# Preparing late weights as planned steps beside group 0, with per-tile waits on released pools

## The chip, the cores and the metric

One Trainium2 chip; the program runs on one of its NeuronCores. The metric is the device time of one execution in microseconds. Before the change the runs gave 2528.05, 2527.34 and 2525.23 us, a median of 2527.34.

A core has five engines that work beside each other, each with its own queue of instructions taken in order: TensorE (PE, matmuls and transposes; PEld is its weight load), VectorE (DVE), ScalarE (ACT), GpSimd (POOL) and SyncE (SP, which here only issues transfers). SPq, ACTq and POOLq in the profile are the issuing sides of SP, ACT and POOL.

## What is computed

Two layers over x of 64 graphs with 256 nodes and 256 features, all in fp32:

```python
x = x + gat(layernorm(x), adj, L0_gnn_W, L0_gnn_a)          # masked softmax attention over the nodes
x = x + mamba2(layernorm(x), W_in, conv, dt, A, D, norm_w, W_out, W_lin, b_lin)
x = x + rgcn(layernorm(x), adj, L1_gnn_weight, L1_gnn_bias) # sums over neighbours, by relation
x = x + moe(layernorm(x), gate_w, gate_b, w1, b1, w2, b2)   # best of 8 experts, capacity 1.25
```

What matters below is the weights. The kernel does not use them as they come. It takes the mean over rows out of W and W_in (so that a layer norm's mean drops out), multiplies the router's weights gate_w, and the columns of W_in that give dt, into the weights of each layer (so that the router's logits and dt come along as a few more columns of products that are made anyway), and folds norm_w, W_out and W_lin into one matrix.

## The kernel before

**First pass.** 16384 tokens are worked on in 32 groups of 512 (two graphs each). A group runs through `attention`, `scan`, `mix` and `relate`; after two groups, `choose` routes their tokens and scatters a record of each into a list in DRAM, `slots`. At its end, two full blocks of the mixture of experts are computed beside the last groups (`first_block`), and `list_blocks` lists the rest. x after the third sum goes to DRAM (`x3d`). **Second pass.** The blocks of the experts that are left are run, in three kinds: quarters (128 tokens), halves (256) and wholes (512), each with its own 1 MB of w1 and of w2. `fetch_slots` reads a block's records, `gather` brings its tokens' rows by indirect transfer from POOL, `fetch_weights` loads the weights, `turned` transposes the rows, `experts` computes. Two blocks' records of each kind and the first block's weights are asked for at once when the pass begins.

**The order within the first pass** is planned in Python while the program is built. `Plan.step` takes an engine, an estimate of its time, a function that issues the instructions, and what it reads and writes. `Plan.record` then simulates the five engines: again and again it picks the step that can begin first, and issues it. Among steps of one engine that can begin within 0.05 us of each other, the lower rank goes first; the rank is `PACE * group + due`, with one due time for each step of a group (`DUE`), and one for each step of the end (`LATE`). The instructions of each engine go out in exactly this order (`manual_schedule`). A tile asked for through the plan (`Plan.tile`) has a number of buffers in turn; a step that needs a buffer waits until all steps of its last use are issued. `AtOnce` has the same interface and issues every step on the spot; a second form of the kernel, for adjacency matrices with entries above 1, is written with it and does not run on this input.

**Preparation of the weights** stands ahead of the plan, in plain program order, in pools of its own, `prep` and `prep_ps` (L514). Its parts, with the lines of the profile:
- ACT issues the load of W_in into `win` (L445) and of small vectors; SP issues the other loads.
- `centred` (L476) takes means out: two products with a matrix of ones, two steps on DVE. It is used for gate_w and the dt columns of W_in (together `gq`), W (`wx`), the three parts of `win`, and the relation's weights (`wrel`).
- `projected` (L488) multiplies a matrix by `gq`: two transposes, a copy (L497), a product (L500), a copy (L504), for each half. It is used for W, `wrel` and W_lin (`wl`).
- Products of W with the attention vectors a (L556, L557), the bias columns (L540), W_out transposed (`woT`, L572) and multiplied by `wl` into `wf` (L579, L583), and b1 transposed and stored in DRAM as `b1d` (L588 to L591).

Attention needs `wx`, `scan` needs `win` and the bias `blin`, `mix` needs `wf`, `relate` needs `wrel` and `brel`, and the expert blocks need `b1d`. When `prep` closes, its memory is released; `fast_pool` and `fast_ps` (L1424), in which all tiles of the first pass lie, are opened over it. In the same way the pools of the second pass (`et`, `es`, `eps`, L1464) are opened over those of the first, the weights' pool `wts` among them. Where a pool is opened over a released one, the first access to it waits for the released pool's last.

Of the kernel before, what the change touches and what calls it, by code (L numbers as in the profile page):

```python
# [31 lines left out]
PACE = 4.60  # L32
DUE = [
    -187, -691, -72, 159, -113, -114, -149, 636, 174, 171, 387, 756, -229, -1087, -1172, 20, -351,
    -599, 699, -611, -1484, 249, -770, -710, -1048, 376, -331, 864, -405, 61, -28, 134, 16, -9,
    348, 442, -429, -1102, -42, 703, -223, 113, -607, 108, 990, 202, 295, 646, 26, 263, -92, 233,
    247, -557, -374, -723, 667, 329, -360, -253, -391, -1223, -304, -600, -778, -988, -488, -62,
    -720, -720, -306, -566, -4, 261, -344, 153, -232, -603, -36, -391, 947, 502, -439, -94, -126,
    29, -246, 327, -208, -945, 61, -486, -490, -648, -49, 120, 553, 10, -408, -1120, -935, -301,
    -1702, 164, -515, 586, -50, -355, 132, 744, -80, 96, -1, 160, -115, 422, 133, 217, -609, 128,  # L40
    -1196, 106, -198, -115, -589, -56, 549, -876, -729, 476, -280, -741, -486, -186, -114, 171,
    711, -911, -300, -262, 1079, -444, -107, -98, 127, 135, -372, -12, -97, 504, 638, 342, -669,
    -318, 1, 363, -806, -1604, -646, -790, 276, -140, 264, -165, 370, 251, 14, -435, -518, -133,
    -470, -615, 98, 237, -148, -214, -868, -1044, -884, 125, 722, 505, 627, 310, 101, 280, 264,
    947, 409, -79, 138, -8, -1018, -924, -303, -515, -328, -216, -660, 755, 133, 127, -181, 129,
    -683, -19, 86, -697, 353, 242, -391, 243, -479, -626, 320, 328, 221, -542, -377, 191, 161,
    -181, 223, -433, -295, 139, 127, 151, -181, 152, -496, -30, 178, -458, 330, 615, -10, 301,
    198, -168, 566, 303, -1378, -203, 504, -349, 138, 15, 93, -300, -469, -71, -1080, -905, -382,
    -765, -499, 522, -559, -436, -711, -1062, -307, -489, 705, -263, 262, 48, 538, -87, -172, -7,
    -532, -975, -688, -187, -1308, -570, 302, -1059, -506, 779, 83, -11, 749, -4, 216, 469, 900,  # L50
    -1142, 86,
]
LATE = [
    439, 482, 387, 262, 460, 193, 260, 587, 397, 193, 239, 309, 207, 431, 312, 489, 501, 247, 320,
    397, 398, 341, 500, 377, 575, 532, 367, 505, 283, 139, 276, 464, 345, 243, 455, 107, 575, 200,
    296, 296, 296, 296, 296, 296, 296, 296, 296, 296, 296, 296, 170, 321, 356, 486, 13, 179, 363,
    192, 357, 768, 395, 1857, 2047, 1812, 2046, 1886, 2036, 1982, 2016, 1957, 1976, 1757, 1937,
    1678, 2042, 1873, 2052, 2162, 2018, 2061, 1964, 2122, 1809, 397, 1880, 2090, 446, 466, 2153,
    1801, 208, 1845, 1887, 420, 371, 1753, 2084, 343, 1955, 1982, 469, 302, 1752, 1929, 128, 2080,
    1921, 332, 270, 332, 389, 145, 449, 139, 514, 497, 334, 177, 408, 502, 1660, 1834, 1843, 1988,  # L60
    2202, 2247, 2273, 2186, 2179, 1985, 1853, 1933, 1944, 2220, 1882, 2133, 1815, 2009, 2179,
    2095, 1789, 1828, 563, 1802, 1733, -146, 109, 1792, 2073, 414, 1763, 1943, 143, 509, 2344,
    2010, 508, 2033, 2085, 250, 423, 2196, 2256, 716, 2018, 1585, 411, 176,
# [56 lines left out]
class Plan:  # L120
# [20 lines left out]

    def tile(self, tag, shape, dtype=F32, bufs=1):
        home = Home(self.pool, tag, shape, dtype, bufs)
        line = self.tags.setdefault(tag, [])

        home.before = (line[-1] if line else None, line[-bufs] if len(line) >= bufs else None)
        line.append(home)
        return home
# [11 lines left out]
    def step(self, engine, us, go, reads, writes, late=0.0):  # L160
        k = self.k.get(self.due, 0)
        self.k[self.due] = k + 1
        due = (DUE if self.due == "group" else LATE)[k]
# [124 lines left out]
def gnn_mamba_rgcn_moe(ctx: ExitStack, tc: tile.TileContext, a: dict, out: bass.AP):  # L288
# [143 lines left out]
    def first_pass(form, pass1):  # L432
# [12 lines left out]
        nc.scalar.dma_start(out=win, in_=a["L0_ffn_W_in"].rearrange("(k p) o -> p k o", p=P))  # L445
# [30 lines left out]
        def centred(pool, banks, dst, src, n):  # L476

            ps = banks.tile([P, 512], F32, tag="ps0", name="ps")
            for k in range(2):
                nc.tensor.matmul(  # L480
                    ps[:, :n], lhsT=ones_pp, rhs=src[:, k, :], start=(k == 0), stop=(k == 1)
                )
            for k in range(2):
                nc.vector.scalar_tensor_tensor(
                    dst[:, k, :], ps[:, :n], -1.0 / D, src[:, k, :], ALU.mult, ALU.add
                )

        def projected(pool, banks, dst, src, n):  # L488

            for k in range(2):  # L490
                ps = banks.tile([P, 512], F32, tag="ps0", name="ps")
                for o in range(2):
                    nc.tensor.transpose(
                        ps[:, o * P : (o + 1) * P], src[:, k, o * P : (o + 1) * P], ident
                    )
                srcT = pool.tile([P, 2 * P], F32, tag="srcT", name="srcT")
                nc.vector.tensor_copy(srcT, ps[:, : 2 * P])  # L497
                ps = banks.tile([P, 512], F32, tag="ps0", name="ps")
                for o in range(2):
                    nc.tensor.matmul(  # L500
                        ps[:, :n], lhsT=srcT[:, o * P : (o + 1) * P], rhs=gq[:, o, :n],
                        start=(o == 0), stop=(o == 1),
                    )
                nc.vector.tensor_copy(dst[:, k, :], ps[:, :n])  # L504

        def relation(pool, banks, dst, r):

            nc.sync.dma_start(
                out=dst[:, :, 0:D], in_=a["L1_gnn_weight"][r].rearrange("(k p) o -> p k o", p=P)
            )  # L510
            centred(pool, banks, dst[:, :, 0:D], dst[:, :, 0:D], D)
            projected(pool, banks, dst[:, :, D:DG], dst[:, :, 0:D], E + 1)

        with tc.tile_pool(name="prep" + form, bufs=1) as prep, tc.tile_pool(  # L514
            name="prep_ps" + form, bufs=2, space=PSUM
        ) as prep_ps:
            own = prep, prep_ps

            w0 = prep.tile([P, 2, D], F32, name="w0")
            nc.sync.dma_start(out=w0, in_=a["L0_gnn_W"].rearrange("(k p) o -> p k o", p=P))  # L520
            gq0 = prep.tile([P, 2, E + 1 + NH], F32, name="gq0")
            nc.vector.memset(gq0[:, :, E : E + 1], 0.0)
            nc.sync.dma_start(
                out=gq0[:, :, 0:E], in_=a["L1_ffn_gate_w"].rearrange("(k p) e -> p k e", p=P)
            )
            nc.vector.tensor_copy(gq0[:, :, E + 1 :], win[:, :, DPROJ - NH :])
            centred(*own, gq, gq0, E + 1 + NH)
            nc.vector.memset(gq[:, :, E : E + 1], -1.0 / D)
            centred(*own, wx[:, :, 0:D], w0, D)
            projected(*own, wx[:, :, D:DQ], wx[:, :, 0:D], E + 1 + NH)  # L530
            for o in range(0, DPROJ - NH, 512):
                part = win[:, :, o : min(o + 512, DPROJ - NH)]
                centred(*own, part, part, min(512, DPROJ - NH - o))
            relation(*own, wrel[:, 0], 0)
            for vec, dst in (("L0_ffn_b_lin", blin), ("L1_gnn_bias", brel)):
                col = prep.tile([P, 2], F32, tag="col", name="col", bufs=2)
                nc.sync.dma_start(out=col, in_=a[vec].rearrange("(k p) -> p k", p=P))
                ps = prep_ps.tile([P, 512], F32, tag="ps0", name="ps")
                for k in range(2):
                    nc.tensor.matmul(  # L540
                        ps[:, : E + 1], lhsT=col[:, k : k + 1].to_broadcast([P, P]),
                        rhs=gq[:, k, : E + 1],
                        start=(k == 0), stop=(k == 1),
                    )
                nc.vector.tensor_copy(dst[:, D:DG], ps[:, : E + 1])

            av = prep.tile([P, 2, D], F32, name="av")
            for i in range(2):
                nc.sync.dma_start(
                    out=av[:, i, :],  # L550
                    in_=a["L0_gnn_a"][i * D : (i + 1) * D, :].rearrange("d o -> o d").broadcast_to([P, D]),
                )
            prod = prep.tile([P, 4, D], F32, name="prod")
            for k in range(2):
                for i in range(2):
                    nc.vector.tensor_mul(prod[:, 2 * k + i, :], wx[:, k, 0:D], av[:, i, :])  # L556
# [1114 lines left out]
```

## Time and profile before

| | us |
|---|---|
| median of 3 runs | 2527.34 |
| profiled execution, its own time | 2531.42 |
| its span (first to last instruction) | 2529.7 |
| PE busy | 2366.6 (94%) |
| DVE busy | 1918.0 (76%) |
| ACT busy | 1641.0 (65%) |
| POOL busy | 826.1 (33%) |

The span is cut into 40 slices of 63 us; a digit is the busy share of a slice in tenths. The last rows are the clock that TensorE was granted, and the DMA engines:

```profile
PE   5899999999999999999999999999884899999996
...
PEclk8999999999999999999999999999997999999998
DMA  3212222322222232222232222222417433333332
```

The first slice and slices 29 to 31 (1830 to 1960 us) differ from the rest. They are the start, and the step from the first pass to the second.

Lines of the timeline give the start, the busy time, the engine, the line of code, the operation with what it writes and reads, the sizes, and in brackets the idle time of the engine just before with what ended it. Rows by stretch give start:end, its length, busy time with number of instructions by engine, the granted clock, the share of the DMA engines' time and GB/s.

### The profile page before, as it was taken

How to read it: one execution, taken by the hardware profiler on the slowest of the kernel's cores; microseconds unless marked ns; L12 is line 12 of the kernel's file. 1: busy time of each engine (PE TensorE's matmuls, PEld its weight loads, DVE VectorE, ACT ScalarE, POOL GpSimd, SP SyncE). 2: the span in 40 equal slices, each digit the busy share in tenths (PEclk: the TensorE clock that was granted, in tenths of full speed). 3: DMA queues.
4: the chain of work that ended last, by engine and by line, in shares of the span. 5: the costliest groups of instructions: out<-in, count | busy, mean ns of one | idle time of the engine just before them, and what ended most of it. 6: DMA issues, size and time to landing. Idle time of an engine off the chain costs nothing.

```text
span 2529.7 us, 35024 instructions
## 1 busy us (share of the span) xinstructions
PE 2366.6 (94%) x11451; PEld 1652.4 (65%) x11451; DVE 1918.0 (76%) x4825; ACT 1641.0 (65%) x3720; POOL 826.1 (33%) x762
## 2 busy tenths in 40 slices
PE   5899999999999999999999999999884899999996
PEld 4567766667667666766766676676654666666664
DVE  3899999999989899999999999999762243344433
ACT  1878888878888787888888888787522223232331
POOL 1122424333342433334343333432523222222231
PEclk8999999999999999999999999999997999999998
DMA  3212222322222232222232222222417433333332
GB/s 113 45 22 57 58 63 62 77 56 53 62 54 70 60 75 54 54 62 64 61 76 57 53 62 53 70 58 44 134 34 264 139 119 116 122 112 108 127 112 64
DMA packets 173527, 198.93 MB, mean 79 GB/s; under 512 B 25448, under 2 KB 157870, under 8 KB 173312
## 3 DMA queue, kind: packets, MB, share of 16 engines
q1 hardware_dynamic: 124816, 135.70, 16.6%
q0 software_dynamic: 46816, 58.88, 12.6%
q8 instruction: 98, 1.61, 0.3%
q10 hardware_dynamic: 1680, 1.79, 0.2%
q14 instruction: 117, 0.96, 0.1%
HBM read 112.47 MB, written 45.45 MB: 62 GB/s over the span
## 4 chain that ended last, share of the span: by engine, by line
DVE 32%; issue 30%; PE 16%; POOL 10%; ACT 8%; DMA 3%; POOLq 0%; SPq 0%; ACTq 0%; DVEq 0%
PE ps L744 11%; DVE y L963 8%; POOL rs L752 4%; POOL xg L409 3%; POOL out_dram L427 3%; DVE gate L946 3%; DVE gate L1108 2%; DVE xh L1105 2%; DMA xg<-x3d,place 2%; DVE st L760 2%; DVE dm L1088 2%; PE ps L1095 1%; DVE ev L857 1%; DVE bm L973 1%; DVE ev L859 1%
## 5 line engine op out<-in xcount | busy, mean ns | idle before, releaser
L744 PE MATMUL ps<-xnT,win 128*128 128x512 f32 x1152 | 542.0, 600 | 4.0 <-ACT xnT L786 4.0
L963 DVE SCALAR_TENSOR_TENSOR y<-ps,cw,y 128x510 f32<-128x510 f32 (+2 forms) x480 | 351.5, 739 | 5.1 <-ACT y L956 3.9
L1030 ACT ACTIVATE dm<-ps,cs 128x256 f32<-128x256 f32 (+1 forms) x1024 | 334.4, 477 | 23.4 <-PE ps L744 22.6
L752 POOL TENSOR_TENSOR rs<-ve,mhalf 128x4 f32<-128x4 f32 x96 | 157.8, 1644 | 562.7 <-DVE ve L750 439.3
L744 PEld LDWEIGHTS ps<-xnT,win 128*128 128x128 f32 x1152 | 204.6, 190 | 170.8 <-issue 157.0
L1563 PE MATMUL ps<-xnT,w 128*128 128x512 f32 (+2 forms) x736 | 280.7, 542 | 13.7 <-DMA w<-in_L_ffn_w_dram 6.9
L1573 PE MATMUL ps<-w,hid 128*128 128x256 f32 x1248 | 276.3, 379 | 0.0
L1573 PEld LDWEIGHTS ps<-w,hid 128*128 128x128 f32 x1248 | 235.3, 190 | 38.7 <-issue 8.6
L744 PE MATMUL ps<-wf,gate 128*128 128x265 f32 x1024 | 252.1, 388 | 0.0
L1563 PEld LDWEIGHTS ps<-xnT,w 128*128 128x128 f32 x736 | 135.7, 200 | 148.4 <-issue 140.6
L1088 DVE TENSOR_TENSOR dm<-dm,bc 128x1536 f32<-128x1536 f32 x128 | 225.8, 1766 | 2.3 <-ACT dm L1036 1.0
L1567 ACT ACTIVATE hid<-ps,b 128x512 f32<-128x512 f32 (+2 forms) x184 | 114.5, 623 | 169.1 <-PE ps L1563 166.7
L744 PEld LDWEIGHTS ps<-wf,gate 128*128 128x128 f32 x1024 | 191.6, 190 | 47.9 <-issue 11.2
L1578 DVE TENSOR_TENSOR yv<-ps,b 128x256 f32<-128x256 f32 x78 | 33.1, 425 | 230.5 <-PE ps L1573 230.5
L1095 PE MATMUL ps<-dm,xdt 128*64 128x256 f32 x1024 | 170.5, 399 | 33.7 <-DVE dm L1088 33.2
L1036 ACT ACTIVATE dm<-dm 128x1536 f32<-128x1536 f32 x128 | 198.6, 1554 | 0.0
L1282 POOL DMA_INDIRECT slots<-meta,sl x128 | 128.0, 1000 | 198.2 <-DVE sl L1279 147.6
L427 POOL DMA_INDIRECT out_dram<-yf,place x78 | 77.9, 999 | 314.1 <-DVE yf L1586 312.9
L760 DVE BATCH_NORM_STATS2 st<-x 128x6 f32<-128x256 f32 x384 | 152.1, 415 | 6.9 <-DMA x<-in_x_dram 6.3
L969 ACT ACTIVATE xh<-y 128x512 f32<-128x512 f32 x160 | 101.2, 632 | 75.5 <-DVE y L963 65.1
L744 PE MATMUL ps<-wh,eT 128*128 128x273 f32 x512 | 142.6, 407 | 7.5 <-ACT eT L882 4.8
L1579 ACT ACTIVATE yv<-yv,meta 128x256 f32<-128x256 f32 x78 | 39.8, 510 | 168.0 <-DVE yv L1578 168.0
(314 smaller groups left out, 5032.4 us busy)
## 6 DMA issues: line engine op xcount, KB each, us to landing
w<-in_L_ffn_w_dram SPq DMA_DIRECT2D x52, 1024.0 KB
x<-blin POOLq DMA_DIRECT2D x32, 530.0 KB
x<-brel POOLq DMA_DIRECT2D x32, 530.0 KB
adji<-in_adj_dram SPq DMA_DIRECT2D x32, 512.0 KB
x<-in_x_dram SPq DMA_DIRECT2D x32, 512.0 KB
x3d<-x SPq DMA_DIRECT2D x32, 512.0 KB
out_dram<-x SPq DMA_DIRECT2D x32, 512.0 KB
cm<-bm SPq DMA_DIRECT2D x32, 128.0 KB
```

The costliest lines, as they stand in the source:

```text
L427: apart("out", nc.gpsimd.indirect_dma_start(out=outf, out_offset=bass.IndirectOffsetOnAxis(ap=col, axis=0), in_=yf, in_offset=None, bounds ...
L744: nc.tensor.matmul(out_, lhsT=lhsT, rhs=rhs, start=(i == 0), stop=(i == len(pairs) - 1))
L752: s.step(POOL, 1.0, lambda: nc.gpsimd.tensor_tensor(rs(), ve(), mhalf[:, 0:4], ALU.pow), [ve], [rs])
L760: s.step(DVE, 0.34, lambda j=j: nc.vector.bn_stats(sb()[:, j, :], src()[:, j, 0:D]), [(src, j)], [(sb, j)])
L963: nc.vector.scalar_tensor_tensor(y3[:, :, d:], p3[:, :, : N - d], cw[:, c, k : k + 1], y3[:, :, d:], ALU.mult, ALU.add,)
L1030: nc.scalar.activation(dm()[:, q, bi, o : o + n], ps()[:, t0 + N - n : t0 + N], AF.Relu, bias=cs()[:, j, h : h + 1], scale=-1.0,)
L1036: s.step(ACT, 1.38, lambda: nc.scalar.activation(dm(), dm(), AF.Exp, scale=-1.0), [], [dm])
L1088: s.step(DVE, 1.67, lambda dm=dm: nc.vector.tensor_mul(dm(), dm(), bc().unsqueeze(1).to_broadcast([P, 2, 2, N + P])), [bc], [dm])
L1095: nc.tensor.matmul(o, lhsT=xdt()[:, 2 * bi, h * 64 : (h + 1) * 64], rhs=dm()[:, q, bi, 0:N], start=True, stop=False,)
L1282: s.step(POOL, 1.1, lambda j=j: apart("slots", nc.gpsimd.indirect_dma_start(out=slots, out_offset=bass.IndirectOffsetOnAxis(ap=sl()[:, j : ...
L1563: nc.tensor.matmul(ps[:, :n], lhsT=w1[:, k, f * P : (f + 1) * P], rhs=xnT[:, k, :], start=(k == 0), stop=(k == 1),)
L1573: nc.tensor.matmul(ps[:, :D], lhsT=hid[:, f, j * P : (j + 1) * P], rhs=w2[:, f, :], start=(f == 0), stop=(f == NFT - 1),)
```

## The change

1. The pools `prep` and `prep_ps` are gone. What they held is parked in tiles that the first pass owns anyway: buffers of `dm` (four of 6 KB per partition, used for the decays in `scan`), and its eight PSUM banks.
2. The preparation is in two functions. `prepare` makes `wx` and `win`. It is issued on the spot, before the plan. `prepare_more` makes `wl`, `wf`, `wrel`, the bias columns and `b1d`. It consists of steps of the plan, of group 0, with due times of their own (`FIRST`), and `Plan.ahead` turns these on.
3. All loads of the preparation go through SP (`win`'s was the first on ACT; ACT keeps those of the small vectors). The dt columns of W_in are loaded on their own (256 runs of 32 bytes) instead of being copied out of `win` on DVE. W and gate_w are loaded where they are used and centred in place.
4. Steps that use `wf`, the relation's weights, a bias or `b1d` name it among what they read, since a planned step now writes it.
5. The pools of the first and the second pass are opened with `reuse_waits="tile"`: an access waits only for the last uses of the released tiles that its own tile lies over.
6. `PACE`, `DUE` and `LATE` have new values.

The core of the diff (tables and the slow form cut):

```diff
-PACE = 4.60
+PACE = 8.50
...
+FIRST = [
+    265, 184, 467, 344, 294, 503, 357, 516, 311, 437, 377, 423, 481, 189, 420, 393, 174, 220, 341,
...
+    def ahead(self):
+        self.g, self.due = 0, "first"
...
-        due = (DUE if self.due == "group" else LATE)[k]
+        due = {"first": FIRST, "group": DUE, "late": LATE}[self.due][k]
...
-        nc.scalar.dma_start(out=win, in_=a["L0_ffn_W_in"].rearrange("(k p) o -> p k o", p=P))
...
+        def spare(s):
+            home = s.tile("dm", [P, 2, 2, N + P], bufs=NCT)
+            def part(o, n):
+                return lambda: home().rearrange("p a b c -> p (a b c)")[:, o : o + n]
+            return home, part
...
+        def prepare(s):
+            one = spare(s)
+            load(s, lambda: wx[:, :, 0:D], a["L0_gnn_W"].rearrange("(k p) o -> p k o", p=P), [(wx_, "W")],
+                 8.0)
+            load(s, lambda: gq[:, :, 0:E], a["L1_ffn_gate_w"].rearrange("(k p) e -> p k e", p=P),
+                 [(wx_, "gq")], 9.0)
+            load(s, lambda: gq[:, :, E + 1 :],
+                 a["L0_ffn_W_in"][:, DPROJ - NH :].rearrange("(k p) e -> p k e", p=P), [(wx_, "qc")], 9.0)
...
+            load(s, lambda: win, a["L0_ffn_W_in"].rearrange("(k p) o -> p k o", p=P), [win_], 15.0)
...
+            for o in range(0, DPROJ - NH, 512):
+                part = win[:, :, o : min(o + 512, DPROJ - NH)]
+                centred(s, part, part, min(512, DPROJ - NH - o), [(win_, o)], [(win_, o)], 1.7)
...
+        def prepare_more(s):
+            one, two, three = (spare(s) for _ in range(3))
...
+            relation(s, wrel[:, 0], 0, s.fixed(wrel))
...
-                accum_op=ALU.add), [], [xe], late=4.5)
+                accum_op=ALU.add), [s.fixed(bias)], [xe], late=4.5)
...
-            pool = pass1.enter_context(tc.tile_pool(name="fast_pool", bufs=1))
-            banks = pass1.enter_context(tc.tile_pool(name="fast_ps", bufs=1, space=PSUM))
+            pool = pass1.enter_context(tc.tile_pool(name="fast_pool", reuse_waits="tile", bufs=1))
+            banks = pass1.enter_context(tc.tile_pool(name="fast_ps", reuse_waits="tile", bufs=1, space=PSUM))
             clear_slots(pool)
             plan = Plan(pool, banks)
...
+            prepare(AtOnce(pool, banks))
+            plan.ahead()
+            prepare_more(plan)
...
-        et = pass2.enter_context(tc.tile_pool(name="et" + form, bufs=2))
+        et = pass2.enter_context(tc.tile_pool(name="et" + form, reuse_waits="tile", bufs=2))
```

`relation` asks for a fourth parking tile in `prepare_more`. `load` is a step on SP that issues one transfer.

## The prediction

> **What bounds the kernel now.** I read the table of slices first (PE 9 tenths or more in nearly all of them), then the busy time by stretch, then the timeline where that table shows PE idle, and last SP's waits. By stretch (start:end, length, then busy PE, PEld, DVE, ACT, POOL, the granted clock, the DMA share and GB/s):
>
> ```profile
> 24.00:45.00 21.00, 16.02 (x61) 12.10 (x60) 7.10 (x20) 0.00 (x0) 0.00 (x0) 0.67 0.02 2
> ...
> 60.00:64.00 4.00, 1.88 (x18) 1.52 (x16) 1.39 (x8) 3.64 (x8) 1.49 (x3) 1.00 0.01 4
> 64.00:68.00 4.00, 0.16 (x3) 0.00 (x0) 3.93 (x5) 2.05 (x5) 0.00 (x0) 0.57 0.08 15
> 68.00:72.00 4.00, 2.61 (x10) 2.22 (x11) 0.39 (x2) 3.54 (x10) 0.00 (x0) 0.50 0.33 116
> ...
> 100.00:1750.00 1650.00, 1599.25 (x8482) 1125.44 (x8480) 1530.53 (x3587) 1365.66 (x3188) 589.41 (x497) 1.00 0.25 58
> ...
> 1895.00:1928.00 33.00, 5.20 (x18) 2.83 (x18) 8.77 (x25) 2.78 (x8) 18.14 (x28) 0.54 0.59 185
> 1928.00:2000.00 72.00, 55.42 (x275) 46.53 (x275) 18.41 (x63) 21.50 (x58) 13.89 (x14) 0.88 0.74 245
> ```
>
> From 100 to 1750 PE is busy 96.9% and DVE 92.8%: little is to be had. Time is lost at the ends of the first pass. From 24 to 45 DMA stands at 0.02 while the weights needed late are made ready, and no group's input is on its way. The timeline (start, busy us, engine, line) says what the first load waits for:
>
> ```profile
> 43.09 0.39 SPq L591 DMA_DIRECT2D b1d<-b1t  x1
> ...
> 45.81 3.95 SPq L803 DMA_DIRECT2D x<-in_x_dram  x5
> ...
> 51.95 1.94 PE L781 MATMUL ps<-ident,x 128*128 128x128 f32 x8 [9.35 <-DMA x<-in_x_dram]
> ```
>
> The x load needs nothing of b1d, but its tile lies in a pool over the released "prep" pool, so it waits for the last access to any prep tile. The second pass shows the same at 1904:
>
> ```profile
> 1901.10 0.97 POOL L427 DMA_INDIRECT out_dram<-y,hide  x1 [1.43 <-DVE y L1402]
> 1903.80 0.18 DVE L1612 TENSOR_SCALAR other<-tested 128x32 f32<-128x32 f32 x1 [2.98 <-DMA out_dram<-y,hide]
> 1904.15 4.55 SPq L1502 DMA_DIRECT2D meta<-slots  x6
> 1906.35 0.19 POOL L405 CAST place<-meta 128x1 int32<-128x1 f32 x1 [4.28 <-DMA meta<-slots]
> ...
> 1927.69 5.71 PE L1563 MATMUL ps<-xnT,w 128*128 128x128 f32 x32 [0.16 <-issue]
> ```
>
> SP has issued nothing since 1840; the last scatter's landing lets it go.
>
> **Start, first half.** Kept ahead of group 0 are wx and win. PE's last matmul that centres win ends at 17.31+5.56 = 22.9, DVE's last step on it at 22.46+1.69 = 24.2. Two small shifts. DVE stalled 1.9 us at 15.46 for aneg, whose load stood on ACT's queue behind win; win goes to SP, so this goes. The new strided load of eight W_in columns (256 runs of 32 B) takes wrel's place at 3.46; the like gate_w load, issued at 2.44, let PE begin at 8.75, 6.3 us later, so PE begins at 3.46+6.3 = 9.8 instead: +1.0. I keep 22.9. Group 0's transposes (51.95) then start at about 22.9: **29 us gained**; DVE's first step on x moves from 51.88 to 24.2, nearly the same.
>
> Will the data be there? SP issues ahead of win cw, cb, W, gate_w, the columns and both halves of av: 0.46+0.52+0.52+0.98+0.98+1.42 = 4.9 from 0.80, so win at about 6.0 with the gaps; it took 6.8 from issue to its first reader (0.81 to 7.64), so 12.8, against 17.3 where PE first needs it. The Trainium skill, "DMA: Bandwidth & Descriptors", section "Issuing engines are not separate DMA queues", says that issuing from several engines saves only the issue time. By that rule the move costs just these 5 us, adji and x are issued by 7.5, and x lands after its 6.05 (45.81 to 51.86) at 13.6. The trace differs: SP's second col load waited 2.2 us for win to land, and ACT's issue of blin came at 7.11, 5.2 after gb's issue ended: only so many transfers are out at once. By the row, adji and x wait for the small loads ahead, aneg's landing at 15.2 being the latest of those, and x lands near 18 to 21. Both are ahead of 22.9, so the sum is the same, but the slack is 2 to 9 us. Ends for this half: 31 and 25.
>
> **Start, second half.** The other steps (wl, woT, wf, wrel, the two bias columns, b1t) are on PE and DVE beside groups 0 to 4. PE's 16.0 us in 24:45 ran at a clock of 0.67; from full-speed rows: wf 16 x 0.246 (252.1/1024) = 3.9, 17 transposes x 0.124 (43.8/352 for L1073) = 2.1, 4 centring products x 0.17 = 0.7, 24 narrow ones at a weight load of 0.19 each = 4.6; sum 11.3. PE's holes from 52 to 84 are 2.1+3.8+1.4+0.5 = 7.9 (the other stretches there are full). If all holes are used, 3.4 is added, if none, 11.3; DVE's 7.1 fit in its idle time there. A rule of the skill would make it cheaper: "TensorE: Matmul & The Clock Gate", Part 1, says that the clock falls to half after an idle window of about 3.4 us. The rows show it, 0.57 and 0.50 in 64:72; filled holes would hold the clock up, and the 6.6 us of PE work in 68:76 would lose about 2.8, leaving 0.6. I take 4, by the rows. **Start: 29-4 = 25**, ends 30 and 14.
>
> Waits that this adds. Preparation parks its data in four "dm" buffers, so group 0's first decay must wait for them: in the trace it comes at 104.61, 52.7 us after the first transposes, while the 16 us of work is over well before; nothing. The bias add (POOL, L791, at 81.88, 30 us after the transposes) now waits for its column; behind it on POOL stands rs L752 of a later group, for which ACT's scaled copies wait. If that slips by 10 us, 10 us are lost in the ramp. First uses of wf and wrel are later still, b1d's is at 1798. The new loads (wo, nw, wl, wrel, cols, b1r) follow x on SP, 1.6 MB before group 1's adji is due. Clearing slots (POOL L615, 0.64 us, and its DMA at 46.14) loses its 40.8 us wait: hidden before and after.
>
> **Second pass.** Waits go tile by tile. Which tile lies over which is in no view; adding up sizes in the order of first request (my assumption), the second quarter's meta lies on the y buffer whose scatter went at 1898.70. The last one, issued at 1901.10, released its reader at 1903.80, so this one would at 1901.4: 2.7 earlier than now. POOL itself is free at 1902.07, 4.3 earlier than its first place step. So in program order on SP: 2.7. If weight loads whose tiles lie over wts come ahead of that meta, about 3 MB move before 1902, at 355 GB/s (1920 to 1940) 8.9 us more of a stretch with 44.4 us of idle PE. Ends 2.7 and 13; I take **7**, as both orders are possible.
>
> **The plan's new order.** Every due time is new and PACE goes from 4.60 to 8.50. A rank only decides between steps that the planner sees starting within 0.05 us, and over five groups in flight PACE adds 34 instead of 18 to dues that span -1534 to 1113. PE's idle 50.8 us in 100:1750 is all there is to win. Bounds: 15 won (a third of it) and 25 lost (half as much again). I take 0: the same steps on the same engines.
>
> **Sum.** 25+7+0 = 32 off the profiled execution, 2531.4 - 32 = 2499. That one stands 4.1 above the median of the runs, so the forecast is **2527.3 - 32 = 2495**.
>
> **Rivals.**
> - Waits by tile buy nothing: SP or POOL still meets a tile of the last scatter. For: SP's queue is in order, and six fetches stand in front. Against: only one of them seems to lie on late data. 2527 - 25 = 2502.
> - Preparation is exposed: PE's holes stay empty, or POOL waits for the bias column. For: steps of preparation come behind groups in rank (174 to 605). Start 14, boundary 4: 2509.
> - All goes well: start 30, boundary 13, order 10: 2474.
> - Slower: the new order makes PE wait more. It must idle 32 us more in 100:1750, that is 82.8, busy 95.0%, or 1.0 us a group over 32 groups; from there on the change loses. At 1.2 a group, 38 lost: 2533. For: DVE at 92.8% leaves little slack, and PE waits there for dm L1088. Against: the limits on rank above.
>
> **Chances.** Forecast 0.38, no gain by tile 0.18, exposed 0.17, all well 0.18, slower 0.06, order eats just the gain 0.03. Measured runs agree to about 0.1%, so 0.2% (5 us) is what can be told from no change. Faster 0.91, same 0.03, slower 0.06. The range goes from 2473 to 2516: below it lies half of "all well" (0.09), above it the tail of "exposed" and the last two (0.12 in all).
>
> **What would show it.** Right: the first transposes of x between 20 and 27; wf's matmuls among groups 0 to 4; PE's holes in the 40 us after that nearly gone; the first meta fetch before 1904 less the gain at the start; PE's idle share from 100 to 1750 still 3%. Wrong: x landing after 27 (the queue), POOL waiting for blin, a meta fetch still released by the last scatter, or PE idle over 80 us in the middle.

## The result, and the profile after

The changed kernel takes **2540.63 us** (median of 4 runs, 2535.91 to 2545.54) against 2527.70 (2525.23 to 2528.55) for the kernel before on the same chip: ratio **1.0049**, interval 1.0028 to 1.0069. It is slower by 13 us, where 32 us less had been forecast. The profiled executions stand closer together, 2535.91 after (the fastest of its runs) and 2531.42 before (above all its timed runs), so the traces have 4.5 us of span to explain (2534.2 against 2529.7), not 13.

First the start. From the timeline of PE, and then of SP, in the changed kernel (start, busy us, engine, line, tiles, and in brackets the idle time before and what ended it):

```profile
19.04 2.07 PE L504 MATMUL ps<-win,tri 128*128 128x512 f32 x2 [7.18 <-DMA win<-in_L_ffn_W_in_dram]
...
28.93 1.10 PE L504 MATMUL ps<-wrel,tri 128*128 128x256 f32 x4 [1.12 <-DMA wrel<-in_L_gnn_weight_dram]
29.87 1.04 PE L839 MATMUL ps<-ident,x 128*128 128x128 f32 x8
```

```profile
6.01 1.48 SPq L552 DMA_DIRECT2D dm<-in_L_gnn_a_dram  x2
7.53 0.43 SPq L552 DMA_DIRECT2D win<-in_L_ffn_W_in_dram  x1
8.01 0.47 SPq L863 DMA_DIRECT2D adji<-in_adj_dram  x1
8.52 12.19 SPq L861 DMA_DIRECT2D x<-in_x_dram  x5
```

The late weights did move: x's first transposes come at 29.87, where they came at 51.95, so the kernel is 22.1 us ahead here. But win, issued at 7.53, reached PE only at 19.04, and in PE's queue the sums for wrel, a weight that is needed late, stand in front of x's transposes.

Win's 256 packets can be told from all others in the trace by their size, 4640 bytes. They move from 12.85 to 18.51; in the kernel before they moved from 2.33 to 6.50, after an issue at 0.81. The two stretches from win's issue to its last packet, in the changed kernel (start:end, length, busy PE, PEld, DVE, ACT, POOL, granted clock, DMA share, GB/s):

```profile
7.53:12.85 5.32, 3.72 (x12) 2.40 (x11) 1.18 (x6) 1.00 (x2) 0.00 (x0) 1.00 0.11 29
12.85:18.51 5.66, 0.00 (x0) 0.00 (x0) 3.37 (x15) 0.00 (x0) 0.00 (x0) 1.00 0.89 348
```

For 5.3 us win stood in the queue while the DMA engines were nearly idle (0.11). The loads in front of it on SP are those of the attention vectors a (`dm<-in_L_gnn_a_dram`), which DVE sees land at 12.87 and 15.56.

What becomes of the lead is seen in the busy time by stretch, each from x's first transposes to 0.3 us into a step of group 5 that DVE starts at 289.61 before and at 280.98 after (mx, the maximum over a row of attention). Before, then after, with the long stretch that the prediction read:

```profile
51.95:289.90 237.95, 227.29 (x1154) 158.07 (x1155) 212.69 (x470) 194.52 (x444) 62.62 (x53) 0.97 0.24 56
```

```profile
29.87:281.30 251.43, 237.95 (x1223) 166.72 (x1222) 223.33 (x484) 193.12 (x443) 58.66 (x53) 0.98 0.21 46
100.00:1750.00 1650.00, 1589.57 (x8377) 1115.50 (x8374) 1538.90 (x3538) 1339.37 (x3137) 589.88 (x494) 0.99 0.26 58
```

The stretch became 13.5 us longer: PE has 10.7 us more to do in it, the late weights, and idles 2.8 us more. 8.6 us of the 22.1 are left at group 5. They are lost to the groups: from mx of group 5 to mx of group 29 a pair of groups takes (1605.62-280.98)/12 = 110.4 us, where it took (1605.38-289.61)/12 = 109.6, and at group 29 the kernel is level (+0.2 us). In 100:1750 PE idles 60.4 us and not 50.8. Over these twelve pairs, which hold the same work, DVE is busy 1236.9 us and not 1217.0. PE's waits in 100:1750 (for what, us in total, times, longest), before and after:

```profile
PE ps L1095 <- DVE dm L1088: 31.9, 14, 2.5
```

```profile
PE ps L487 <- DVE run L1318: 26.9, 14, 2.1
PE ps L1153 <- DVE dm L1146: 12.8, 13, 1.7
```

The wait for dm became smaller, and a wait for run, the router's running counts, came in: 2 us once in each pair. Another 8 us go in the last groups and the first blocks (the last store of x3d is 8.0 us later than before), and 3.5 us come back in the second pass. At the boundary to the second pass the timeline of the changed kernel shows:

```profile
1908.03 0.97 POOL L436 DMA_INDIRECT out_dram<-y,hide  x1 [1.42 <-DVE other L1676]
...
1910.65 3.77 SPq L1566 DMA_DIRECT2D meta<-slots  x5
```

One meta fetch did go early, at 1882.33. The other five still follow the last scatter: 2.62 us from its issue to theirs, where it was 3.05.

### The profile page after: what moved, and what is told of

It reads as the page before. It is cut to its first block, busy times and chain, and to the rows that moved or that the text cites. A ratio compares the mean times of both kernels' runs of the same rounds, so it can differ in the third digit from the quotient of the medians.

```text
span 2534.2 us, 35008 instructions
## 1 busy us (share of the span) xinstructions
PE 2368.3 (93%) x11451; PEld 1651.4 (65%) x11451; DVE 1942.7 (77%) x4824; ACT 1635.3 (65%) x3720; POOL 829.8 (33%) x762
## 3 DMA queue, kind: packets, MB, share of 16 engines
q0 software_dynamic: 46816, 58.88, 12.8%
## 5 line engine op out<-in xcount | busy, mean ns | idle before, releaser
L487 PE MATMUL ps<-xnT,win 128*128 128x512 f32 x1152 | 554.2, 608 | 1.8 <-ACT dm L1088 0.8
L1021 DVE SCALAR_TENSOR_TENSOR y<-ps,cw,y 128x506 f32<-128x506 f32 (+2 forms) x480 | 347.0, 737 | 3.6 <-ACT y L1014 3.3
L810 POOL TENSOR_TENSOR rs<-ve,mhalf 128x4 f32<-128x4 f32 x96 | 164.5, 1714 | 562.2 <-DVE ve L808 458.7
L1153 PE MATMUL ps<-dm,xdt 128*64 128x256 f32 x1024 | 167.6, 393 | 16.4 <-DVE dm L1146 13.5
L1171 POOL TENSOR_TENSOR xh<-xh 128x512 f32<-128x512 f32 x64 | 93.7, 1472 | 182.9 <-ACT xh L1168 180.7
```

What stands on the lines that cost most here:

```text
L487: nc.tensor.matmul(out_, lhsT=lhsT, rhs=rhs, start=(i == 0), stop=(i == len(pairs) - 1))
L810: s.step(POOL, 1.0, lambda: nc.gpsimd.tensor_tensor(rs(), ve(), mhalf[:, 0:4], ALU.pow), [ve], [rs])
L1021: nc.vector.scalar_tensor_tensor(y3[:, :, d:], p3[:, :, : N - d], cw[:, c, k : k + 1], y3[:, :, d:], ALU.mult, ALU.add,)
L1153: nc.tensor.matmul(o, lhsT=xdt()[:, 2 * bi, h * 64 : (h + 1) * 64], rhs=dm()[:, q, bi, 0:N], start=True, stop=False,)
```

## The experiments

The result and the experiments were taken on five chips: the kernel before takes 2527 us on that of the result, 2545 on that of e7 to e10, and 2484 on the three of all other runs. Each time is therefore read as a ratio to the kernel before on the same chip; where an expectation counts in us, they are from 2527. The ratios (interval):

| run | what is in it | ratio |
|---|---|---|
| e1_old_tables | change, PACE, DUE, LATE of before | 0.9976 (0.9968 to 0.9985) |
| e2_new_tables | before, with the three new tables | 1.0206 (1.0189 to 1.0223) |
| e3_old_late | change, LATE of before | 1.0115 (1.0092 to 1.0138) |
| e4_ahead | change, late weights ahead of the plan | 1.0161 (1.0144 to 1.0178) |
| c_after, c_after2 | the change itself | 1.0117 (1.0100 to 1.0133), 1.0108 (1.0091 to 1.0124) |
| e5_old_due | change, PACE and DUE of before | 0.9965 (0.9952 to 0.9977) |
| e6_run_late | change, run reckoned 2 us later | 1.0202 (1.0185 to 1.0219) |
| e9_win_first | e5 and win loaded first | 0.9967 (0.9954 to 0.9979) |
| e10_no_tile | e5 without tile waits in pass 2 | 0.9957 (0.9941 to 0.9974) |
| e13_wrel_late | e9 and wrel behind x on PE | 0.9948 (0.9931 to 0.9964) |

**Old tables in the changed kernel, new tables in the old one.** Only the numbers are exchanged; what is computed, and by which steps, stays.

```
-PACE = 8.50
+PACE = 4.60
-DUE = [ -145, -616, ...      (and LATE; FIRST stays)
+DUE = [ -187, -691, ...
```

> The changed kernel with PACE, DUE and LATE of the kernel before (FIRST kept). Theory A, the new order is the cause: group 0 to 4 keep most of the lead of 13 to 20 us that the changed kernel has at its first stores, groups 28 and 29 do not lose 10 us, the first pass ends near 1890 instead of 1908, and the time is 2505 to 2520, below both kernels. Rival B, the preparation beside group 0 is the cause: the lead is lost all the same and the time is 2535 to 2545. Rival C, the lead is lost to a limit of the steady state (PE at 97%), whatever the order: 2522 to 2528.

> The kernel before with PACE, DUE and LATE of the changed one, preparation in its own pools as before. Theory A: slower than before by what the changed kernel lost after its start, 15 to 25 us, so 2543 to 2553, with PE waiting for the running counts of the router (DVE run) every second group. Rival B: 2525 to 2530, as before.

> The changed kernel with LATE alone as before; PACE and DUE stay new. If the 10 us lost between 1690 and 1790 come from the due times of the end, about 2530; if they come from those of the groups, 2538 to 2542, and E1 and this one differ by all of it.

The new tables alone cost the old kernel 2% (51 us of 2484, about twice the most that theory A had), with 21.8 us of PE waiting for run between 300 and 1600. The change with the old tables is faster than before, though by 6 us only: in its ratio it lies between the ranges of theory A and of rival C. The pair of groups decides. It takes 106.3 us in e1_old_tables, as in the kernel before on such a chip, and a lead of 8.9 us at group 5 is still 8.9 at group 29. So the loss in the groups comes from **the order, not the moved preparation**; what is lost of the lead ahead of group 5 is lost with either table. LATE has no part in it: with it put back the ratio is that of the changed kernel (c_after).

**The late weights issued ahead of the plan**, at once, and not as its steps:

```
-            plan.ahead()
-            prepare_more(plan)
+            prepare_more(AtOnce(pool, banks))
```

> The changed kernel with the second half of the preparation issued on the spot, ahead of the plan, instead of as steps of it. By the prediction's sum this half costs 4 us beside the groups and, ahead of them, its 16 to 20 us of before: 2552 to 2560. If the start's lead is lost in the ramp whatever its size (rival C), the time is within 5 us of the changed kernel, 2536 to 2546.

1.0161, against 1.0115 of e3_old_late on the same chip and 1.0117 of the changed kernel: as steps beside group 0 the same work costs 10 to 11 us less, even in the new order (12 to 20 had been expected).

**The two kernels unchanged on a chip of 2484, and PACE and DUE put back alone.**

> The kernel before, unchanged, to have its trace on the chip on which the order was tried. If the old order has two steady regimes (with PE waiting about 2.4 us for dm once per pair of groups, as in the first trace, or without it), a time near 2484 goes with less than 10 us of PE waiting for dm between 300 and 1600, and a time near 2527 with about 29 us. Ratio 1.000.

> The changed kernel, unchanged, on this chip. The order is the cause (theory A): its PE waits for run here as on the first chip (about 21 us between 300 and 1600), so its time stays near 2520 to 2545, and against a before of 2484 it is 1.015 to 1.025. The order is not the cause (rival): 1.003 to 1.007 as on the first chip.

> The changed kernel with PACE and DUE of before, LATE new. Theory A with the loss in the dues of the groups: the wait for run is gone, within 0.2% of the kernel with all old tables (0.9976): 0.995 to 1.001. If it takes LATE as well (with LATE alone put back the ratio was 1.0115): about 1.006 to 1.012.

The kernel before gave 1.0000 (0.9991 to 1.0009), without the wait for dm. On such a chip the change costs 1.2%, between theory A's range and the rival's, and PACE and DUE are all of it: from 1.0117 to 0.9965, 38 us. The old order needs 106.3 us for a pair of groups, with or without the moved preparation, and the new order 109.0. The first pass is 32.7 us longer at group 29 (1588.9 against 1556.2) and 39.8 at the last store of x3d, so the loss at its end belongs to the order too.

**Run reckoned later.** If the wait for run is only badly placed work on PE, telling the planner that run is ready 2 us later should put PE's product behind it.

```
-                op(0.08, lambda j=j: v.tensor_add(
-                    run()[:, j + 1, :], run()[:, j, :], oh()[:, j, :]), [oh], run)
+                s.step(DVE, 0.08, lambda j=j: v.tensor_add(
+                    run()[:, j + 1, :], run()[:, j, :], oh()[:, j, :]), [oh], [run],
+                    late=2.0 if j == 6 else 0.0)
```

> The changed kernel with all new tables; the planner alone is told that the last of the seven running counts is ready 2.0 us later than it reckons, so it puts PE's product with run (and what hangs on it) later in PE's queue. If the wait for run (about 2 us in every pair of groups, some 30 us over 16 pairs) is what the new order costs, most of it goes: 1.003 to 1.010 here where the changed kernel gives about 1.02. If that wait only stands in for another limit that the order has, another wait takes its place and it stays within 0.3% of the changed kernel.

The product moved back, the wait for run went, and a longer one took its place: 1.0202 is worse than either case had it. PE's waits between 300 and 1600 in this kernel:

```profile
PE ps L1046 <- DVE da L989: 31.4, 11, 3.3
```

So DVE as a whole is late at this place, not run alone. The next view shows why. It is the timeline of DVE and POOL at one pair of groups, in the changed kernel (c_after2) and then in the kernel before (c_before), both on chips of 2484:

```profile
920.79 0.21 DVE L1302 TENSOR_TENSOR lg<-lg,rs 128x64 f32<-128x64 f32 x1
920.92 2.52 DVE L986 TENSOR_SCALAR dv<-dv 128x32 f32<-128x32 f32 x1
921.03 2.45 DVE L1303 TENSOR_TENSOR lg<-lg,gb 128x64 f32<-128x64 f32 x1
921.46 0.71 POOL L1295 COPY meta<-rs 128x8 f32<-128x8 f32 x1
921.61 1.78 POOL L1171 TENSOR_TENSOR xh<-xh 128x512 f32<-128x512 f32 x1
923.52 0.22 DVE L1304 TENSOR_REDUCE lmx<-lg 128x8 f32<-128x64 f32 x1
...
926.74 1.87 DVE L915 SCALAR_TENSOR_TENSOR ev<-ev 128x1024 f32<-128x1024 f32 x1
```

```profile
916.55 2.23 POOL L1237 COPY meta<-rs 128x8 f32<-128x8 f32 x1
...
917.13 0.22 DVE L1245 TENSOR_TENSOR lg<-lg,gb 128x64 f32<-128x64 f32 x1
...
917.53 1.22 DVE L857 SCALAR_TENSOR_TENSOR ev<-ev 128x1024 f32<-128x1024 f32 x1
917.86 3.46 POOL L1113 TENSOR_TENSOR xh<-xh 128x512 f32<-128x512 f32 x2
918.66 0.74 DVE L963 SCALAR_TENSOR_TENSOR y<-ps,cw,y 128x510 f32<-128x510 f32 x1
919.32 0.78 DVE L1247 TENSOR_TENSOR lg<-lg,lmx 128x64 f32<-128x64 f32 x1
```

In the new order two small DVE steps, 0.2 us each, take 2.5 us together and end at 923.44 and 923.48, when POOL's addition of squares does (921.61+1.78 = 923.39). The router's step lg<-lg,gb is held so in each of the first 14 pairs (2.45 us or more in 13 of them, 1.32 in one), dv<-dv, which stands ahead of it, in eight. In the old order the router's same step is through before POOL's addition starts. There it is POOL that is held, its 128x8 copy until 918.78, while DVE's ev runs to 918.75. The DVE step that lies beside the addition and reads PSUM (y<-ps,cw,y) keeps its 0.74 us; lg<-lg,lmx behind it takes 0.78, where it takes 0.22 in the new order. The Trainium skill, "SBUF — State Buffer", section "SBUF: two separate sides", has a rule for this: DVE and GpSimd share one pair of ports as an exclusive lock, which a DVE step needs if it has two SBUF inputs (against a GpSimd instruction that reads SBUF) or runs in a two-port mode; whichever starts first keeps it for its whole instruction, and the other is blocked fully. The traces agree that one is blocked until the other ends, DVE in the new order (until 0.05 and 0.09 us after the addition) and POOL in the old (0.03 us after ev); in which mode dv<-dv runs they do not show. Which one started first they do not show: the records of the held DVE steps begin 0.6 to 0.7 us before that of the addition, and that of POOL's copy 0.98 us before ev. The hold-up is 2.2 us a pair, about as long as PE's wait for run, which ends at 937.30 in this pair (so some 14 us later, not 5, as the next expectation has it). Two experiments were to show that it is the cause.

**The held instruction left out.** The router's addition of the gate's bias becomes an empty step, in the new order and, as e8_no_gb_old, in the old one.

```
-            op(0.14, lambda: v.tensor_add(lg(), lg(), gb.unsqueeze(1).to_broadcast(e3)), [], rows)
+            op(0.14, lambda: None, [], rows)
```

> The changed kernel in its own order, step for step, with one DVE instruction left out in each pair of groups: the router's addition of the gate's bias (lg<-lg,gb; the bias is zero in this input, so the routing stays). In the traces of the new order this instruction takes 2.45 us where it takes 0.23 in the old one, and ends each time when POOL's copy of xh ends; PE's wait for run, 2 us a pair, follows 5 us later. Theory A': the new order costs its time because DVE comes to that place just behind POOL and is held until POOL is done. Then 2.2 us a pair go, 16 pairs, about 30 us: ratio 1.000 to 1.004 where the changed kernel gave 1.0117, no wait for run left. Rival (DVE's hold-up is hidden, or the next DVE instruction is held in its place): 1.009 to 1.012.

> The same instruction left out of the kernel with the old PACE and DUE (ratio 0.9965), where it takes 0.23 us and DVE has work beside it. By theory A' nothing to gain: 0.995 to 0.998. If leaving it out gives 10 us or more here too, what the run before shows is a shorter router and not the hold-up.

This was badly chosen twice. The bias is not zero in the runs: the routing changed, the second pass had 98 output steps (yf<-fin,yv) and not 78, and the ratios of 1.0578 and 1.0486 say nothing of the order. And the first pass shows the rival right. From the timeline of e7_no_gb, at two pairs:

```profile
825.74 0.18 DVE L986 TENSOR_SCALAR dv<-dv 128x32 f32<-128x32 f32 x1
825.86 0.22 DVE L1304 TENSOR_REDUCE lmx<-lg 128x8 f32<-128x64 f32 x1
826.17 2.12 DVE L977 TENSOR_SCALAR s<-u 128x32 f32<-128x32 f32 x1
```

```profile
937.74 2.52 DVE L986 TENSOR_SCALAR dv<-dv 128x32 f32<-128x32 f32 x1
937.86 2.40 DVE L1304 TENSOR_REDUCE lmx<-lg 128x8 f32<-128x64 f32 x1
938.17 2.12 DVE L977 TENSOR_SCALAR s<-u 128x32 f32<-128x32 f32 x1
938.44 1.78 POOL L1171 TENSOR_TENSOR xh<-xh 128x512 f32<-128x512 f32 x1
```

In eight of the first 14 pairs dv<-dv, ahead of the step left out, is held as before, and the reduction behind it ends with it (both at 940.26). In the other six dv<-dv and the reduction pass in 0.2 us each, and s<-u behind them is held. So another DVE step is held in the place of the one left out; the reduction is in none of these pairs held by itself. It is POOL's instruction that must go.

**POOL's additions left out**, as empty steps, so that the order stays: the norm then holds a quarter of its squares.

```
-                    s.step(POOL, 1.45, lambda c=c: nc.gpsimd.tensor_add(
-                        sq()[:, c, :], sq()[:, c, :], sq()[:, c - 1, :]), [(xh, c - 1)], [(xh, c)])
-            s.step(POOL, 1.4, lambda: nc.gpsimd.tensor_add(
-                sq()[:, 3, :], sq()[:, 3, :], sq()[:, 1, :]), [(xh, 1)], [(xh, 3)])
+                    s.step(POOL, 1.45, lambda c=c: None, [(xh, c - 1)], [(xh, c)])
+            s.step(POOL, 1.4, lambda: None, [(xh, 1)], [(xh, 3)])
```

> The changed kernel again, as the control of the next two: its ratio here (1.005 on one chip, 1.012 on another) and the time of a pair of groups between group 5 and group 29 (about 109.0 to 109.5 us, 106.3 in the old order on a chip on which it never waits).

> The changed kernel in its own order, with POOL's three additions of squares per group (xh<-xh, 128x512) left out, so the norm's sum holds a quarter of the squares and the blocks of the second pass may differ: only the first pass is read, as time of a pair of groups against the control. Theory A' (the new order puts the router's small DVE steps right behind one of these additions, DVE is held for it, 2.2 us a pair, whichever DVE instruction stands there): no DVE instruction of the router stays above 1 us, PE's wait for run goes, and a pair gets at least 1.5 us shorter than in the control. Rival (the order is limited by something else, such as where PE's products stand): a pair stays within 0.5 us of the control, and PE waits for run as before.

> The same additions left out of the kernel with the old PACE and DUE. Theory A': they lie beside DVE work that they don't hold up, so a pair stays within 0.5 us of that kernel's 106.2 us on a chip on which it never waits (110.7 where DVE's xdt is late). If a pair gets shorter by 1.5 us here too, POOL's additions cost any order the same and do not tell the two orders apart.

The router's held step, by tile (shortest, median and longest in ns, first and last start), in c_after2, e11_no_add and c_before:

```profile
L1303 DVE TENSOR_TENSOR lg<-lg,gb x16: 211/2454/2517, 268.6 to 1828.8; 128x64 f32<-128x64 f32 x16
```

```profile
L1301 DVE TENSOR_TENSOR lg<-lg,gb x16: 218/226/430, 265.5 to 1776.1; 128x64 f32<-128x64 f32 x16
```

```profile
L1245 DVE TENSOR_TENSOR lg<-lg,gb x16: 224/226/844, 279.4 to 1800.0; 128x64 f32<-128x64 f32 x16
```

And PE's wait for run between 300 and 1600, in c_after2 and in e11_no_add:

```profile
PE ps L487 <- DVE run L1318: 23.0, 12, 2.1
```

```profile
PE ps L487 <- DVE run L1316: 0.6, 1, 0.6
```

Without the additions a pair in the new order takes (1542.03-274.83)/12 = 105.6 us, 3.3 less than in the control ((1588.02-280.80)/12 = 108.9). In the old order it takes 105.8, 0.5 less than its 106.3. Without POOL's additions the two orders are equally fast; with them the new one is 2.6 us a pair slower. POOL has less to do in these runs too, but as much less in the old order, which gains only the 0.5. **Theory A' holds** in this. The whole times (0.9979 and 0.9988) are not read: the second pass has 81 output steps here and not 78.

One point of theory A' is wrong: DVE's work is held up in the old order too. The same twelve pairs by busy time, in c_before, c_after2, e12_no_add_old and e11_no_add:

```profile
289.24:1564.68 1275.44, 1265.82 (x6745) 893.00 (x6744) 1214.64 (x2881) 1079.81 (x2532) 482.33 (x408) 1.00 0.27 64
280.80:1588.02 1307.22, 1277.26 (x6746) 899.38 (x6745) 1237.63 (x2882) 1080.66 (x2532) 486.52 (x408) 0.99 0.27 62
279.09:1548.89 1269.80, 1264.55 (x6746) 893.04 (x6745) 1188.56 (x2881) 1084.66 (x2532) 394.94 (x336) 1.00 0.27 64
274.83:1542.03 1267.20, 1263.30 (x6747) 894.57 (x6746) 1192.27 (x2882) 1087.63 (x2533) 390.19 (x336) 1.00 0.28 64
```

POOL's additions make DVE busy 45.4 us longer in the new order and 26.1 us longer in the old one: 3.8 and 2.2 us a pair. In the new order ev<-ev is among the held steps, once a pair (1.87 us above, 1.22 in the old order and without the additions). What tells the orders apart in time is whether PE waits behind the held steps: it idles 30.0 us in the new order and 9.6 in the old one, 3.9 and 5.3 without the additions. That is 20.3 of the 31.8 us by which the new order is longer. The other 11.4 us are PE's own busy time for the same matmuls, at a granted clock of 0.99 and not 1.00; they go with the additions as well, but what makes them was not tested.

**Win first, and wrel behind x.** Both with the old PACE and DUE. In the first, win's load goes back to the head of ACT's queue; in the second the planner is also told that wrel's load takes 20 us, so that PE comes to wrel later.

```
+        nc.scalar.dma_start(out=win, in_=a["L0_ffn_W_in"].rearrange("(k p) o -> p k o", p=P))
-            load(s, lambda: win, a["L0_ffn_W_in"].rearrange("(k p) o -> p k o", p=P), [win_], 15.0)
...
-            s.step(SP, 3.0, lambda: nc.sync.dma_start(      (second run only)
+            s.step(SP, 20.0, lambda: nc.sync.dma_start(
```

> The kernel with the old PACE and DUE, and win's load issued first, on ACT's queue as before the change, and not behind seven loads on SP. In the changed kernel PE waits 6.7 to 7.2 us for win (it lands at 19.0). If that wait sets when x's transposes begin, they come about 6 us earlier and the time falls by 3 to 7 us: ratio 0.9935 to 0.9955. If x's own landing, or the ramp of the groups, takes it back: 0.996 to 0.998.

> The kernel with old PACE and DUE and win's load first (0.9967), with the planner told that wrel's load takes 20 us instead of 3, so that PE's sums for wrel stand behind x's transposes. In the run without this PE waited 9.8 us for wrel to land (27.48) ahead of x's transposes (29.32). If that is what keeps them late, they come at 18 to 22 and the first pass ends 5 to 9 us earlier: ratio 0.993 to 0.995. If x lands later than that or the ramp takes it back: 0.9955 to 0.9975.

PE's timeline in e9_win_first, then in e13_wrel_late:

```profile
27.48 2.04 PE L505 MATMUL ps<-wrel,tri 128*128 128x256 f32 x4 [9.82 <-DMA wrel<-in_L_gnn_weight_dram]
29.32 1.81 PE L839 MATMUL ps<-ident,x 128*128 128x128 f32 x8
```

```profile
19.48 1.87 PE L839 MATMUL ps<-ident,x 128*128 128x128 f32 x8 [2.19 <-DVE win L513]
```

With win first nothing is gained, because PE then waits for wrel: its load stands behind x's on SP, and its step before x's on PE. With both, x's transposes start at 19.48, the first pass is about 7 us ahead of e5_old_due from group 5 to group 29, and the ratio is 0.9948, as expected. This version beats both kernels: 2470.31 us where the kernel before takes 2483.89 and the changed one 2511.11 on the same chip. Its interval still overlaps that of e5_old_due.

**The tile waits of the second pass taken back**, in the kernel with the old PACE and DUE:

```
-        et = pass2.enter_context(tc.tile_pool(name="et" + form, reuse_waits="tile", bufs=2))
+        et = pass2.enter_context(tc.tile_pool(name="et" + form, bufs=2))
```

and likewise for es and eps.

> The kernel with the old PACE and DUE, and the three pools of the second pass waiting for the whole released pool again, as before the change. If the tile waits are worth the 7 us of the prediction, 0.9990 to 1.0000; if they are worth the 0.4 us that the gap between the last scatter and the next fetch shows (2.62 against 3.05), 0.996 to 0.9975.

0.9957, its interval ending at 0.9974. On the same chip e9_win_first, which has the tile waits, takes 2536.3 us and this kernel 2535.7, although its last store of x3d comes 3.2 us later. So a gain of 7 us from the tile waits is excluded, and no gain at all can be seen.

## Why the prediction was wrong

- **The step that failed: "I take 0: the same steps on the same engines."** The order was costed by what the planner can see, a rank between steps within 0.05 us of each other. The planner knows nothing of two engines excluding each other. Which DVE step lies beside which POOL step is therefore left to the tables, and the same steps cost 2.6 us more a pair: 36 to 38 us on a chip where the old order hardly waits. Even the bound of 25 us was too small there, since PE's idle time was taken as the reserve, and no DVE step was expected to change its length. The rival named a wait for dm and a price of 1.0 us a group; its sign was right, but not the wait, and it had 6 of 100.
- **"I keep 22.9" for x's transposes: 29.87.** Win was reckoned to land at 12.8 and came at 19.04. By the rule that the prediction cites, its move to SP costs the time of the issues ahead of it; the measured delay is longer. It was issued only 1.5 us later than reckoned, but its first packet moved 5.3 us after that (1.5 in the kernel before), and the packets then took 5.7 us (4.2 before), with adji and x issued right behind it and not, as the prediction had it, behind small loads. That win stood behind the loads of a on SP's queue is read from the order of issue; at the head of ACT's queue, in e9_win_first, its packets move from 2.28 to 6.11. Behind win stood wrel on PE, which the prediction did not see in the queue. That x itself can be there by 18 to 21 was right with win in front: e13_wrel_late transposes it at 19.48. The half is worth 22, not 29.
- **"I take 4" for the second half: 13.5.** The work itself was sized well (10.7 us more of PE, 11.3 reckoned). The holes of the ramp were not used up; PE idles 2.8 us more after the transposes. The start as a whole is worth 8.6 and not 25, which the runs with the old order confirm from end to end: 0.9976 and 0.9965, or 6 and 9 us.
- **"I take 7" for the tile waits: about 0.4.** The second of the six meta fetches still follows the last scatter, and the four behind it on SP's queue follow with it; whether these wait for late data themselves cannot be seen. The rival that gave the tile waits nothing, with SP's order as its reason, was right in this.
- **Hidden, as forecast:** the bias add. POOL releases none of PE's longer waits between 29.87 and 281; the longest, 4.1 us, is for ACT's adji.

The sum on the chip of the result, from the two traces: 8.6 won at the start, 8.9 lost from group 5 to group 29, 7.7 lost from there to the last store of x3d, 3.5 won in the second pass. That is 4.5 us lost, where 32 won had been forecast.

The loss is smaller there (1.0049) than on the chips of 2484. The likely reason is that the old order waits there as well: 31.9 us for dm, of which the new order has 12.8. The moved preparation without the new order was not run on that chip; on the chip of 2545, where PE has the same wait, e9_win_first and e10_no_tile, which differ from it by one point each, gave 0.9967 and 0.9957.

## What to carry to other kernels

A planner's due times are not neutral: before a new table is costed at nothing, look in the trace at which DVE steps lie beside POOL's long instructions, and price those of the kinds that were held here (two inputs in SBUF, or a TENSOR_SCALAR in SBUF; the reduction was not) at POOL's full duration, if the engine that limits the kernel waits behind them. A step that suddenly takes ten times its length and ends with another engine's instruction is a hold-up, and leaving that step out only hands it to another. And when a weight's preparation is moved, look at both queues: a load can stand behind others of its queue while the DMA engines are nearly idle (win, 5.3 us), and a load behind x on SP with its step before x on PE puts the weight back in front.

## What the runs showed of the hardware

The same program is not equally fast on every chip: the kernel before took 2484 us on three chips, 2527 and 2545 on two. One place was found in the traces where they differ. On the slow chips DVE does not start the four steps xdt one after the other, while POOL issues the eight scatters to slots beside them. DVE's timeline before, on the chip of 2527, and then on a chip of 2484:

```profile
312.52 0.69 DVE L1078 TENSOR_TENSOR xdt<-ps,dt 128x512 f32<-128x512 f32 x1
314.56 0.69 DVE L1078 TENSOR_TENSOR xdt<-ps,dt 128x512 f32<-128x512 f32 x1 [1.35 <-PE ps L744]
316.01 0.69 DVE L1078 TENSOR_TENSOR xdt<-ps,dt 128x512 f32<-128x512 f32 x1 [0.76 <-PE ps L744]
```

```profile
312.12 1.89 DVE L1078 TENSOR_TENSOR xdt<-ps,dt 128x512 f32<-128x512 f32 x3
```

PE had the data ready on both (its 16 transposes start at 311.88 on the first and at 311.49 on the second, and take 1.91 us), so the releaser that the view names is not the cause. The dm that follows starts at 318.80 and not at 315.56, PE waits 2.5 us for it, and with it the old order takes 109.6 us a pair and not 106.3. What holds DVE there on some chips and not on others stays open; no experiment was made on it.
